# Inner products of a Strassen-Winograd FFN kernel on one core: one more third-level pair, two input tiles summed by a load, small operations and quarter products in another place

## The chip, the cores and the metric

The kernel runs on one core of a Trainium2 chip. Its engines work in parallel, each through its own list of instructions in order: TensorE (PE in the profile, with its weight loads as PEld) multiplies matrices into PSUM banks, VectorE (DVE) and GpSimd (POOL) do elementwise arithmetic, ScalarE (ACT) applies functions and copies, and SyncE (SP) only issues transfers. POOL issues transfers as well, by a queue of its own, and each such issue stands in POOL's list between its other instructions. Instructions of different engines wait for each other by semaphores. The metric is the device time of one execution, in microseconds (us); lower is better.

## The reference

The kernel computes two layers with residuals on x of shape (32, 128, 2048), float32. In each, a conditioned mixing of the channels feeds a feed-forward part:

```
def L0_cond(x, embedding, ...):
    att = softmax(mlp(embedding))                      # (32, 8)
    agg_w = einsum('bk,koi->boi', att, weight)
    agg_b = att @ bias_k
    return einsum('boi,bih->boh', agg_w, x) + agg_b[:, :, None]
def L0_ffn(x, W, bias, A, Bf, coeffs, scales):
    out = einsum('bsd,od->bso', x, W) + bias           # x as (32, 128, 2048), W (2048, 2048)
    return out + einsum('ebsr,eor,e->bso', einsum('bsd,erd->ebsr', x, A), Bf, coeffs * scales)
def L1_cond(x, c, weight, c_weight, bias):
    out = conv1d(x, weight, groups=4, taps=9)
    return out + (c @ c_weight.T)[:, :, None] + bias[None, :, None]
def L1_ffn(x, up, down, perm):
    t = x[..., perm] in 16 heads of 128
    return (gelu(t @ up[head]) @ down[head])[..., unperm]
x = x + L0_ffn(L0_cond(x, cond, ...), ...)
x = x + L1_ffn(L1_cond(x, cond, ...), ...)
```

What this case is about is the first large product, x with the 2048x2048 matrix W (into which the low-rank update of A and Bf has been added), for 32x128 = 4096 rows.

## The kernel before

**The product and its rounds.** The product of x and W is cut in halves on all three sides and done by a scheme of seven products in place of eight. The seven outer products are the rounds, in the order `ROUNDS` P1, P2, P6, P7, P5, P3, P4. Each needs one combination of W's quarters and one of x's. A round goes over 8 steps g = 0 to 7, one for each group of four batches, so there are 56 steps; "step 17" is round P6 with g = 1. Within a step the same scheme is used once more: the step's matrices are cut again, seven inner products, also named P1 to P7, are made, and each is added into the quarters of the step's result.

**One step on PE.** One inner product is four matmuls (128x128 weights by 128x512), which the profile shows as 8 records of one half each, 0.429 us apart; a product thus takes 3.43 us. A plain step, `multiply` (L331), makes all seven products. In the pairs of steps that `PAIRS` (L51) lists, `multiply_third` (L426) is used instead: each of the two steps makes five products itself (P1, P5, P6, P3, P7, at L445), and the remaining two of both steps together are made by a third level of the scheme, as seven "quarters" (L458), each of 8 records of 128x256. All quarters run in the pair's odd step. `turn` places them: with `early` true they come between the five products, two after P1, two after P5, two after P6, one after P3; with `early` false they come behind the five. In the rounds P1 and P4 (`ENDS`) they come behind, in the others between. After a pair's odd step, the results of both steps are stored from SP (L275). Pair numbers are g // 2.

**Reading of banks.** Each product accumulates in a PSUM bank. After P1 has been written, VectorE adds the bank into the step's results (L438 for the third-level step, one addition for each of up to two results); P6 and P7 go on accumulating in that same bank, so they may begin only when the addition before has read it. The quarters' additions are at L466.

**Inputs of a step.** `x_loads` (L283) issues the loads of x's tiles (1 MB each) from SP, two steps ahead at the top of a step; for steps of P6 at the fourth of the six calls of `between` in the step. `x_combine` (L294), one step ahead, makes the combination on POOL. Its `pieces` (L277) are four POOL operations of 128x512 each: for P6 it makes x10 + x11 and from this takes x00, which is eight operations, and stores the outcome to the scratch s2 by POOL's own queue; for P5 it makes x10 + x11 alone. Then follow four operations that make the inner combinations s (L309 to L312): s[0] is used by inner P5, s[1] by P6, s[2] by P7, s[3] by P3. Inner P1 uses the combination itself. The tiles live in a pool of 26 slots of 1 MB, and a load waits until its slot is free.

**Other work on POOL and VectorE.** `inner_weights` (L243), 16 POOL operations, makes a round's inner weights in the last step of the round before. `outer_weights` (L520) loads and combines a round's outer weights in steps g = 2 to 6 of the round before. `third_weights` (L378) makes the quarters' weights: part on POOL at the first pair of a round, the others (`quarter_ops`) on VectorE at calls of `between`. `third_inputs` (L410) makes the quarters' inputs sq by four operations; on VectorE in pair 0 of a round and in all pairs of P6, right after the even step, else on POOL in the even step (L1079). `mixed_kernel` (L553) puts two VectorE operations of the mixed weights into each of the first four calls of `between`.

**The loop.** One pass of the loop at L1068 issues step i. On POOL the order of a pass is: the combination of step i+1, sq if it is POOL's, the inner weights if g = 7, the outer combination. Then the step's products run, with `between(0)` to `between(5)` among them.

**The small chain.** `small()` (L876) computes softmax, the bias `aggb` (8 VectorE operations, L931 to L935), `ctxb` and `ctx34` (four small matmuls and five VectorE operations, L938 to L945), the scaled row sums and the convolution's weights, cut in parts by `yield`; each pass of the loop takes one part, from step 5 on two. `aggb` and `ctxb` are first read after the seven rounds.

After the rounds comes a phase with the layers' remaining parts and the 16 heads' FFN (from L1180), which the change does not touch.

Of the kernel before, what the change touches and what calls it, by code (L numbers as in the profile page):

```python
# [11 lines left out]
ALU = mybir.AluOpType  # L12
# [4 lines left out]
P = 128  # L17
B = 32
L = 2048
QW = 512  # L20
KEXP = 8
GR = 4
# [26 lines left out]


PAIRS = {  # L51
    "P1": (1, 2, 3), "P2": (0, 1, 2), "P6": (0, 1, 2, 3), "P7": (0, 1, 2, 3),
    "P5": (0, 1, 2, 3), "P3": (0, 1, 2, 3), "P4": (0,),
}
ENDS = ("P1", "P4")
# [3 lines left out]
def adaln_ffn_kernel(  # L59
# [16 lines left out]
    nc = tc.nc  # L76
# [12 lines left out]
    def bank():  # L89
        return banks.pop(0)  # L90

    def done(*ps):
        banks.extend(ps)

    def halves(t):
        return [t[:, r * NQ : (r + 1) * NQ] for r in range(2)]
# [23 lines left out]
    att_bc = const.tile([P, B * KEXP], FP, name="att_bc", tag="att_bc")  # L120
    aggb = const.tile([P, B], FP, name="aggb", tag="aggb")
    ctxb = const.tile([P, GR, B], FP, name="ctxb", tag="ctxb")
    ctx34 = const.tile([P, GR, B], FP, name="ctx34", tag="ctx34")
# [140 lines left out]
    def x_load(g, tp, kh):  # L264
        t = slot(f"xt_{g}{tp}{kh}", (P, 2, 2, QW))
        nc.sync.dma_start(t.rearrange("p k s c -> p (k s c)"), xT[g, tp, kh])
        return t
# [9 lines left out]
    def pieces(out, a, b, op):  # L277

        for i in range(2):
            for j in range(2):  # L280
                nc.gpsimd.tensor_tensor(out[:, i, j], a[:, i, j], b[:, i, j], op)  # L281

    def x_loads(r, g):  # L283
        return {
            "P1": lambda: [x_load(g, 0, 0)],
            "P2": lambda: [x_load(g, 0, 1)],
            "P6": lambda: [x_load(g, 1, 0), x_load(g, 1, 1), x_load(g, 0, 0)],
            "P7": lambda: [x_load(g, 0, 0), x_load(g, 1, 0)],
            "P5": lambda: [x_load(g, 1, 0), x_load(g, 1, 1)],
            "P4": lambda: [x_load(g, 1, 1)],  # L290
            "P3": lambda: [x_load(g, 0, 1), part_load("s2", g)],
        }[r]()

    def x_combine(r, g, ts):  # L294

        a = ts[0]
        tt = nc.gpsimd.tensor_tensor
        if r == "P6":

            b, a, c = ts  # L300
            pieces(b, b, a, ALU.add)
            pieces(a, b, c, ALU.subtract)
            part_store("s2", g, a)
        if r in ("P7", "P5", "P3"):
            pieces(a, a, ts[1], ALU.add if r == "P5" else ALU.subtract)
        xa[steps.index((r, g))] = a
        s = slot(f"s_{r}{g}", (P, 4, QW))
        a11, a12, a21, a22 = a[:, 0, 0], a[:, 1, 0], a[:, 0, 1], a[:, 1, 1]
        tt(s[:, 0], a21, a22, ALU.add)  # L309
        tt(s[:, 1], s[:, 0], a11, ALU.subtract)  # L310
        tt(s[:, 2], a11, a21, ALU.subtract)
        tt(s[:, 3], a12, s[:, 1], ALU.subtract)  # L312
        return {
            "P1": a11, "P2": a12, "P3": s[:, 3], "P4": a22,
            "P5": s[:, 0], "P6": s[:, 1], "P7": s[:, 2],
        }
# [109 lines left out]
    def multiply_third(r, g, lhs, rhs, olds, between, quarters, sq):  # L426

        px, py = bank(), bank()
        accs = olds if olds[0] is not None else [slot(f"m_{r}{g}", (P, 2, 2, QW))]
        fresh = set()  # L430
        if sq:
            both = [held.pop(), accs]

        def add(si, oi, ps):
            for acc in accs:
                to = acc[:, si, oi]
                if olds[0] is not None or (si, oi) in fresh:
                    nc.vector.tensor_tensor(to, ps, to, ALU.add)  # L438
                else:
                    nc.scalar.copy(to, ps)  # L440
            fresh.add((si, oi))

        def product(k, ps, first, last):
            for kc in range(4):
                nc.tensor.matmul(  # L445
                    ps, lhsT=lhs[k][:, bass.ts(kc, P)], rhs=rhs[k][kc],
                    start=first and kc == 0, stop=last and kc == 3, skip_group_check=True,
                )

        def quarter(k, to):  # L450

            if k in ("P1", "P5", "P2"):
                qs[k] = bank()
            ps = qs[{"P6": "P1", "P7": "P1", "P4": "P1", "P3": "P5"}.get(k, k)]
            first, last = k in ("P1", "P2", "P5"), k in ("P2", "P3", "P4")
            for i, out in enumerate(halves(ps)):
                for kc in range(2):
                    nc.tensor.matmul(  # L458
                        out, lhsT=sq[k][:, i, bass.ts(kc, P)], rhs=quarters[i][k][kc],
                        start=first and i == 0 and kc == 0, stop=last and i == 1 and kc == 1,  # L460
                        skip_group_check=True,
                    )
            b, h = to
            for acc in both[b]:
                part = acc[:, :, 0, h * NQ : (h + 1) * NQ]
                nc.vector.tensor_tensor(  # L466
                    part, ps.rearrange("p (s n) -> p s n", s=2), part, ALU.add
                )
            if last:
                done(ps)  # L470

        qs = {}
        turns = [
            (("P1", (0, 0)), ("P2", (0, 0))), (("P6", (0, 1)), ("P5", (1, 1))),
            (("P7", (1, 1)), ("P3", (0, 1))), (("P4", (1, 0)),),
        ]

        def turn(n, now):
            if sq and now:
                for k, to in turns[n]:  # L480
                    quarter(k, to)

        early = r not in ENDS
        product("P1", px, True, False)
        add(0, 0, px)
        between(0)
        turn(0, early)
        product("P5", py, True, False)
        add(1, 1, py)
        between(1)  # L490
        turn(1, early)
        product("P6", px, False, False)
        add(0, 1, px)
        between(2)
        turn(2, early)
        product("P3", py, False, True)
        add(0, 1, py)
        done(py)
        between(3)
        turn(3, early)  # L500
        product("P7", px, False, True)
        add(1, 1, px)
        add(1, 0, px)
        done(px)
        turn(0, not early)
        between(4)
        turn(1, not early)
        turn(2, not early)
        between(5)
        turn(3, not early)  # L510
        if not sq:
            held.append(accs)
            return
        for b, accs in enumerate(both):
            for (_, new), acc in zip(ADDED[r], accs):
                part_store(new, g - 1 + b, acc, nc.sync)
# [359 lines left out]
    def small():  # L876
# [7 lines left out]
        cond_s, w0, b0s, w1, b1s, w2, b2s, bk, cw, fb = (take(P, n) for _, n in SMALLS)  # L884
# [42 lines left out]
        nc.tensor.matmul(p3[:, : B * KEXP], lhsT=ones[0:B], rhs=adiag, start=True, stop=True)  # L927
        nc.vector.tensor_copy(att_bc, p3[:, : B * KEXP])
        done(p3)
        ab = att_bc.rearrange("p (b k) -> p b k", k=KEXP)  # L930
        nc.vector.tensor_scalar(aggb, ab[:, :, 0], bk[:, 0:1], None, ALU.mult)  # L931
        for k in range(1, KEXP):
            nc.vector.scalar_tensor_tensor(
                aggb, ab[:, :, k], bk[:, k : k + 1], aggb, ALU.mult, ALU.add
            )  # L935

        yield
        for r in range(GR):  # L938
            p4 = bank()
            nc.tensor.matmul(  # L940
                p4[:, :B], lhsT=cw[:, r * P : (r + 1) * P], rhs=cond_s, start=True, stop=True
            )
            nc.vector.tensor_scalar(ctxb[:, r], p4[:, :B], fb[:, r : r + 1], None, ALU.add)
            done(p4)
        nc.vector.tensor_scalar(ctx34, ctxb, 0.75, None, ALU.mult)  # L945
        yield

        while len(made) < 16:
# [58 lines left out]
        for g in range(NG):  # L1007
            nc.vector.tensor_scalar(orow[:, g], pos, g * L, None, ALU.add)
            if g % 2 == 1:
                yield  # L1010


    ctx.enter_context(tc.manual_schedule())
# [4 lines left out]
    steps = [(r, g) for r in ROUNDS for g in range(NG)]  # L1018
# [14 lines left out]
    xs = {0: [x_load(0, 0, 0)]}  # L1033
# [22 lines left out]
    rhs = inner_weights("P1", first, make_first)  # L1056
# [4 lines left out]
    nxt, waiting, ts, quarter_ops = {}, {}, {}, []  # L1061
# [6 lines left out]
    for i, (r, g) in enumerate(steps):  # L1068
# [13 lines left out]
        if i + 1 < len(steps) and not last_round and i != NG - 1:  # L1082
            olds_load(i + 1)
        ahead = i + 2 < len(steps) and ri > 0 and not last_round
        if ahead and steps[i + 2][0] != "P6":
            xs[i + 2] = x_loads(*steps[i + 2])
        if g == NG - (1 if ri else 2) and ri < len(ROUNDS) - 1:
            nxt = inner_weights(ROUNDS[ri + 1], [nxt[kc] for kc in range(4)])
# [36 lines left out]
        def between(j):  # L1125

            b = (ri - 1) * (NG - 2) + g + 1 if ri > 0 else g - (NG - 2)
# [6 lines left out]
                nc.vector.tensor_tensor(*quarter_ops.pop(0), ALU.subtract)  # L1134
            if i == NG - 1 and j == 3:
                olds_load(i + 1)
            if j == 3 and ahead and steps[i + 2][0] == "P6":
                xs[i + 2] = x_loads(*steps[i + 2])
            if ri == 0 and j in (1, 3) and unsummed:
                row_sums(*unsummed.pop())  # L1140
            if ri == 0 and j == 5 and unsummed_first:
                t = unsummed_first.pop(0)
# [33 lines left out]
        if g == NG - 1 and ri + 1 < len(ROUNDS):  # L1176
            rhs = nxt
# [3 lines left out]
    for k, (g, h) in enumerate(heads):  # L1181
# [5 lines left out]
        t = ts.pop(k)  # L1187
# [77 lines left out]
```

## Time and profile before

| quantity | value |
|---|---|
| median of three runs | 2590.43 us (2590.31 to 2591.47) |
| the profiled execution's own time | 2593.28 us |
| its span in the profile | 2591.5 us |
| mean granted PE clock | 0.998 |
| PE's idle time before L458, released by L466 | 3.3 us, once |
| PE's idle time before L221, released by L224 | 3.1 us in two waits, the longest 2.8 |
| a step of round P2 by `multiply` | 24.03 us |
| an even and an odd step by `multiply_third` | 17.17 and 29.25 us |

The span is one execution as the profiler recorded it, from its first to its last instruction; the execution's own time is a little longer than the span. A row of the profile names the line, the engine, the operation, then output and inputs with the tile names, and the number of instructions. A timeline row begins with the start in us from the span's beginning and the length of the group; in square brackets stand the idle time of that engine directly before it, and what ended it. A DMA row gives the size of a transfer and the median time from its issue to its landing. The two steps of a third-level pair differ in length because the odd one also runs the seven quarters.

### The profile page before, as it was taken

Reading aid. Unit: us, or ns where it says so; the run is one execution under the profiler, and the core shown is the slowest. Engines: PE = TensorE matmul, PEld = TensorE weight load, DVE = VectorE, ACT = ScalarE, POOL = GpSimd, SP = SyncE. Lnnn points to the kernel's source line nnn. Section 1 sums busy time; section 2 is a strip of 40 time slices with the busy share of each in tenths; the row PEclk is TensorE's granted clock in tenths of the full one; section 3 lists DMA queues with packets and bytes.
Section 4 is the critical chain, followed back from the end, with each engine's and each line's share of the span. In section 5 each row is a group of like instructions: output and inputs, shape, how many; then the busy total and the mean of one; then the engine's idle time right before and its main releaser. Section 6 shows DMA issues by size and latency. Waiting matters only on the chain. (4 is left out here: it accounts for less than half of the span.)

```text
span 2591.5 us, 21761 instructions
## 1 busy us (share of the span) xinstructions
PE 2576.1 (99%) x7022; PEld 1335.3 (52%) x7022; DVE 1512.9 (58%) x2373; ACT 532.4 (21%) x1099; POOL 1369.4 (53%) x1128
## 2 busy tenths in 40 slices
PE   9999999999999999999999999999999999999999
PEld 4455555455555555555554554555545554455543
DVE  5665565466555667544376666667666666666601
ACT  0000000000000000000011244444444444444432
POOL 7431766989977935968523234343444334434222
PEclk9999999999999999999999999999999999999999
DMA  7452458779366477474767788877777877787532
GB/s 324 177 211 97 179 219 325 280 311 365 158 258 284 164 316 321 181 311 163 247 233 247 241 299 263 250 238 230 223 234 236 258 231 221 226 256 233 162 128 89
DMA packets 186577, 608.30 MB, mean 235 GB/s; under 512 B 17632, under 2 KB 91872, under 8 KB 142304
## 3 DMA queue, kind: packets, MB, share of 16 engines
q1 hardware_dynamic: 147936, 473.48, 51.0%
q0 software_dynamic: 32704, 130.04, 14.9%
q10 hardware_dynamic: 5824, 3.40, 0.4%
q8 instruction: 56, 0.92, 0.1%
q14 instruction: 57, 0.47, 0.1%
HBM read 372.45 MB, written 200.84 MB: 221 GB/s over the span
## 5 line engine op out<-in xcount | busy, mean ns | idle before, releaser
L835 PE MATMUL bank<-t,ws 128*128 128x512 f32 x1024 | 460.3, 592 | 0.0
L846 PE MATMUL bank<-gl,ws 128*128 128x512 f32 x1024 | 460.1, 592 | 0.0
L853 POOL DMA_INDIRECT out<-t,orow x128 | 152.4, 1191 | 540.8 <-DVE t L851 472.2
L838 ACT ACTIVATE gl<-bank 128x512 f32<-128x512 f32 x512 | 305.9, 598 | 417.6 <-PE bank L835 414.4
L445 PE MATMUL bank<-P_t,s_P 128*128 128x512 f32 x736 | 326.6, 592 | 0.0
L846 PEld LDWEIGHTS bank<-gl,ws 128*128 128x128 f32 x1024 | 194.6, 190 | 233.0 <-issue 231.5
L835 PEld LDWEIGHTS bank<-t,ws 128*128 128x128 f32 x1024 | 194.6, 190 | 226.6 <-issue 222.9
L584 POOL TENSOR_TENSOR x<-x,fb 128x512 f32<-128x512 f32 x128 | 176.1, 1405 | 231.5 <-DMA x<-in_x 134.2
L851 DVE TENSOR_TENSOR t<-bank,t 128x512 f32<-128x512 f32 x128 | 88.4, 691 | 325.2 <-PE bank L846 325.2
L438 DVE TENSOR_TENSOR u<-bank,u 128x512 f32<-128x512 f32 x204 | 134.0, 687 | 239.3 <-PE bank L445 223.8
L590 ACT ACTIVATE bank<-w,aggb 128x512 f32<-128x512 f32 x128 | 80.8, 683 | 869.0 <-DMA w<-w_d 856.7
L445 PE MATMUL bank<-wo_P,s_P 128*128 128x512 f32 x544 | 241.6, 592 | 0.0
L281 POOL TENSOR_TENSOR xt<-xt,xt 128x512 f32<-128x512 f32 x128 | 164.0, 1314 | 113.6 <-DMA xt<-in_xT 113.6
L445 PEld LDWEIGHTS bank<-P_t,s_P 128*128 128x128 f32 x736 | 139.8, 190 | 159.8 <-issue 155.7
L563 DVE SCALAR_TENSOR_TENSOR ags<-mix,att_bc,ags 128x128 f32<-128x128 f32 x224 | 174.9, 781 | 4.7
L309 POOL TENSOR_TENSOR s_P<-xt 128x512 f32<-128x512 f32 x56 | 73.7, 1316 | 194.0 <-DMA xt<-in_xT 181.0
L445 PEld LDWEIGHTS bank<-wo_P,s_P 128*128 128x128 f32 x544 | 103.4, 190 | 116.5 <-issue 113.8
L819 POOL DMA_INDIRECT t<-hx_d,row x128 | 132.3, 1033 | 57.4 <-issue 24.9
L458 PE MATMUL bank<-P_q,sq 128*128 128x256 f32 x552 | 129.2, 385 | 3.4 <-DVE u L466 3.3
L458 PEld LDWEIGHTS bank<-P_q,sq 128*128 128x128 f32 x552 | 106.6, 194 | 35.6 <-issue 20.6
L438 DVE TENSOR_TENSOR p<-bank,p 128x512 f32<-128x512 f32 x84 | 56.7, 689 | 113.7 <-PE bank L445 113.7
L445 PE MATMUL bank<-wo_P,xt 128*128 128x512 f32 x272 | 122.3, 592 | 0.0
(190 smaller groups left out, 3525.6 us busy)
## 6 DMA issues: line engine op xcount, KB each, us to landing
xt<-in_xT SPq DMA_DIRECT2D x88, 1024.0 KB, 11.8
u<-u_d SPq DMA_DIRECT2D x40, 1024.0 KB, 10.2
wo_P<-wb_d SPq DMA_DIRECT2D x36, 1024.0 KB, 13.8
u<-c_d SPq DMA_DIRECT2D x64, 512.0 KB, 7.1
x<-in_x SPq DMA_DIRECT2D x32, 1024.0 KB, 9.2
xg<-x SPq DMA_DIRECT2D x256, 128.0 KB, 5.5
hx_d<-x1t SPq DMA_DIRECT2D x32, 1024.0 KB, 6.0
hx_d<-ht SPq DMA_DIRECT2D x32, 1024.0 KB, 7.2
```

What stands on the lines that cost most here:

```text
L281: nc.gpsimd.tensor_tensor(out[:, i, j], a[:, i, j], b[:, i, j], op)
L438: nc.vector.tensor_tensor(to, ps, to, ALU.add)
L445: nc.tensor.matmul(ps, lhsT=lhs[k][:, bass.ts(kc, P)], rhs=rhs[k][kc], start=first and kc == 0, stop=last and kc == 3, skip_group_check=True,)
L458: nc.tensor.matmul(out, lhsT=sq[k][:, i, bass.ts(kc, P)], rhs=quarters[i][k][kc], start=first and i == 0 and kc == 0, stop=last and i == 1 ...
L563: nc.vector.scalar_tensor_tensor(ag, mix[:, k], att, ag, ALU.mult, ALU.add)
L584: nc.gpsimd.tensor_tensor(xt[:, f], xt[:, f], late["fb"][:, f], ALU.add)
L819: nc.gpsimd.indirect_dma_start(out=t.rearrange("p k t -> p (k t)"), out_offset=None, in_=hx_d[g].rearrange("l k t -> l (k t)"), in_offset= ...
L835: nc.tensor.matmul(pu, lhsT=w[:, m * P : (m + 1) * P], rhs=t[:, 0], start=True, stop=True)
L838: nc.scalar.activation(gl[m], pu, AF.Gelu)
L846: nc.tensor.matmul(pd, lhsT=w[:, (MC + m) * P : (MC + m + 1) * P], rhs=gl[m], start=(m == 0), stop=(m == MC - 1),)
L851: nc.vector.tensor_tensor(t[:, 1], pd, t[:, 1], ALU.add)
L853: nc.gpsimd.indirect_dma_start(out=out, out_offset=bass.IndirectOffsetOnAxis(ap=orow[:, g, h : h + 1], axis=0), in_=t[:, 1], in_offset=None,)
```

## The change

There are four edits.

1. `PAIRS["P2"]` gets pair 3, so that steps g = 6 and 7 of round P2 go by `multiply_third`.
2. In P6 and P5, x10 + x11 is no longer made by POOL operations from two loaded tiles. x10 is loaded by SP; a transfer from POOL's queue then reads x11 from memory and adds it onto the loaded tile (`accum_op=add`). `x_add` puts this transfer into a list, which is issued at `between(1)`, that is behind the pass's other POOL work. P6 loads two tiles by SP in place of three and runs four pieces in place of eight; P5 loads one in place of two and runs none. P6's loads move from `between(3)` to the top of the step two ahead, where the others are.
3. The operations of `aggb`, `ctxb` and `ctx34` move to the end of `small()`, two at a time between `yield`s; what stood behind them comes one or two parts earlier.
4. `early` is false in all of P6 and wherever the pair's odd step has g = 1: the quarters of these pairs come behind the five products.

```diff
@@ -49,7 +49,7 @@
 PAIRS = {
-    "P1": (1, 2, 3), "P2": (0, 1, 2), "P6": (0, 1, 2, 3), "P7": (0, 1, 2, 3),
+    "P1": (1, 2, 3), "P2": (0, 1, 2, 3), "P6": (0, 1, 2, 3), "P7": (0, 1, 2, 3),
@@ -280,13 +280,21 @@
+    pending = []
+
+    def x_add(t, g, tp, kh):
+        pending.append(lambda: nc.gpsimd.dma_start(
+            t.rearrange("p k s c -> p (k s c)"), xT[g, tp, kh], accum_op=ALU.add
+        ))
+        return t
+
...
-            "P6": lambda: [x_load(g, 1, 0), x_load(g, 1, 1), x_load(g, 0, 0)],
+            "P6": lambda: [x_add(x_load(g, 1, 0), g, 1, 1), x_load(g, 0, 0)],
...
-            "P5": lambda: [x_load(g, 1, 0), x_load(g, 1, 1)],
+            "P5": lambda: [x_add(x_load(g, 1, 0), g, 1, 1)],
@@ -297,12 +305,10 @@
         if r == "P6":
 
-            b, a, c = ts
-            pieces(b, b, a, ALU.add)
-            pieces(a, b, c, ALU.subtract)
+            pieces(a, a, ts[1], ALU.subtract)
             part_store("s2", g, a)
-        if r in ("P7", "P5", "P3"):
-            pieces(a, a, ts[1], ALU.add if r == "P5" else ALU.subtract)
+        if r in ("P7", "P3"):
+            pieces(a, a, ts[1], ALU.subtract)
@@ -480,7 +486,7 @@
-        early = r not in ENDS
+        early = r not in ENDS and r != "P6" and g != 1
@@ -927,14 +933,79 @@
         nc.vector.tensor_copy(att_bc, p3[:, : B * KEXP])
         done(p3)
+        yield
...
         ab = att_bc.rearrange("p (b k) -> p b k", k=KEXP)
         nc.vector.tensor_scalar(aggb, ab[:, :, 0], bk[:, 0:1], None, ALU.mult)
         for k in range(1, KEXP):
             nc.vector.scalar_tensor_tensor(
                 aggb, ab[:, :, k], bk[:, k : k + 1], aggb, ALU.mult, ALU.add
             )
-
-        yield
+            if k % 2 == 1:
+                yield
         for r in range(GR):
...
             done(p4)
+            if r % 2 == 1:
+                yield
         nc.vector.tensor_scalar(ctx34, ctxb, 0.75, None, ALU.mult)
         yield
@@ -1082,7 +1091,7 @@
         ahead = i + 2 < len(steps) and ri > 0 and not last_round
-        if ahead and steps[i + 2][0] != "P6":
+        if ahead:
             xs[i + 2] = x_loads(*steps[i + 2])
@@ -1134,8 +1143,10 @@
-            if j == 3 and ahead and steps[i + 2][0] == "P6":
-                xs[i + 2] = x_loads(*steps[i + 2])
+            if j == 1:
+                for add in pending:
+                    add()
+                pending.clear()
```

More of the change, by code (lines that the diff above doesn't have):

```diff
@@ L929, in small @@
         done(p3)
[L930 to L935, printed above, removed]
-        yield
[L938 to L945, printed above, removed]
         yield
@@ L1010, in small @@
                 yield
+        ab = att_bc.rearrange("p (b k) -> p b k", k=KEXP)
+        nc.vector.tensor_scalar(aggb, ab[:, :, 0], bk[:, 0:1], None, ALU.mult)
+        for k in range(1, KEXP):
+            nc.vector.scalar_tensor_tensor(
+                aggb, ab[:, :, k], bk[:, k : k + 1], aggb, ALU.mult, ALU.add
+            )
+            if k % 2 == 1:
+                yield
+        for r in range(GR):
+            p4 = bank()
+            nc.tensor.matmul(
+                p4[:, :B], lhsT=cw[:, r * P : (r + 1) * P], rhs=cond_s, start=True, stop=True
+            )
+            nc.vector.tensor_scalar(ctxb[:, r], p4[:, :B], fb[:, r : r + 1], None, ALU.add)
+            done(p4)
+            if r % 2 == 1:
+                yield
+        nc.vector.tensor_scalar(ctx34, ctxb, 0.75, None, ALU.mult)
+        yield
     ctx.enter_context(tc.manual_schedule())
```

## The prediction

> **What bounds the kernel now.** First the page's busy table, to see which engine sets the time; then PE's waits, since only they can be removed on a busy PE; then DVE's and PE's timelines around the two long waits, the granted clock in windows there, and POOL's timeline where P6 begins.
>
> ```profile
> span 2591.5 us, 21761 instructions
> PE 2576.1 (99%) x7022; PEld 1335.3 (52%) x7022; DVE 1512.9 (58%) x2373; ACT 532.4 (21%) x1099; POOL 1369.4 (53%) x1128
> ```
> PE works 2576.1 of 2591.5 us: a change gains by fewer PE instructions or by its 15.4 us of idle time, and loses by any new wait of PE.
>
> ```profile
> PE bank L458 <- DVE u L466: 3.3, 1, 3.3
> PE bank L221 <- DVE w L224: 3.1, 2, 2.8
> ```
> Two waits (total, times, longest) are long. DVE's timeline (start, length) shows what was ahead of L224 for the second, PE's the first:
> ```profile
> 208.17 0.28 DVE L931 TENSOR_SCALAR aggb<-att_bc,small 128x32 f32<-128x32 f32 x1
> 208.48 4.97 DVE L933 SCALAR_TENSOR_TENSOR aggb<-att_bc,small,aggb 128x32 f32<-128x32 f32 x7
> ...
> 213.37 2.47 DVE L224 TENSOR_TENSOR w<-bank,w 128x512 f32<-128x512 f32 x4
> ```
> ```profile
> 884.33 3.60 PE L445 MATMUL bank<-P_t,s_P 128*128 128x512 f32 x8
> 891.25 6.47 PE L458 MATMUL bank<-P_q,sq 128*128 128x256 f32 x16 [3.33 <-DVE u L466]
> ```
> The windows around the latter (PE busy first, PEclk, the granted clock, third from the end):
> ```profile
> 885.00:890.00 5.00, 2.92 (x7) 0.95 (x5) 4.96 (x6) 0.00 (x0) 5.00 (x5) 1.00 0.14 57
> 890.00:895.00 5.00, 3.75 (x9) 3.06 (x10) 4.96 (x8) 0.00 (x0) 4.84 (x5) 0.51 0.00 2
> ```
> A wait costs more than its length: the clock halves behind it, record by record for 6.8 us here and 3.4 us behind the 2.8 us wait at 211. Waits of 0.46 to 0.88 show no drop. POOL where P6's first inputs are made:
> ```profile
> 458.07 9.82 POOL L281 TENSOR_TENSOR xt<-xt,xt 128x512 f32<-128x512 f32 x8 [14.83 <-DMA xt<-in_xT]
> ...
> 494.81 11.18 POOL L281 TENSOR_TENSOR xt<-xt,xt 128x512 f32<-128x512 f32 x8
> 506.29 0.57 POOL L275 DMA_DIRECT2D s_d<-xt  x1 [0.30 <-POOL xt L281]
> 506.88 1.27 POOL L309 TENSOR_TENSOR s_P<-xt 128x512 f32<-128x512 f32 x1
> ```
> ```profile
> 505.54 3.60 PE L445 MATMUL bank<-wo_P,xt 128*128 128x512 f32 x8
> ```
> Step 17 (P6, g=1) starts at 505.54 with P1; its P5 needs s0 of L309, done at 508.15, and is due at 508.98. POOL is 53% busy on the mean, but here has 0.8 us to spare.
>
> **The change, part by part.**
>
> *Third level in P2's last pair.* PE's timeline gives a plain pair 488.38 − 440.31 = 48.07 us and a third-level pair 393.89 − 347.47 = 46.42: gain **1.65**. Its sq costs POOL four operations of 1.27 = 5.1 us, startable when PE's last quarter of the pair before ends (436.9). It ends by 442, hidden under POOL's present 14.83 us wait to 458; without that cover all 5.1 would go into P6's chain below.
>
> *Biases at the end.* The 8 DVE operations (5.25 us) leave the place ahead of L224. Summing what PE's records take above the pitch there gives 2.96 for the wait and gap, 0.49 behind it, and three later 0.42: **4.7** gained. At their new place they come two by two, about 1.4 us of DVE at a step's end in steps 15 to 17, with four small matmuls that only change place. DVE (58% busy) hides them; uncovered, one pair delays a bank's reading by at most 1.4.
>
> *Late quarters.* At P5's g=1, wait and half clock exceed the pitch by 3.49+0.34+11×0.21+0.20 = 6.3. With quarters behind, PE runs P1, P5, then P6 at 884.33, which needs P1's two adds read. Those stand behind sq's four operations on DVE (1.11, 1.64, 1.76, 1.75; ended 886.19 in the timeline), so they end at 887.4: a residue of 3.0, and with the 2.6 of clock little gained (0.7). At the first operation's 1.11 each, sq ends at 884.5 and the adds at 885.7: residue 1.3, gain 5.0. I take **5.0**, as POOL's four pieces of P5 that ran beside sq are gone. P6's g=1 has three small excesses, 0.17+0.19+0.10 = **0.46**. In pair 0 of P2, P7 and P3 the P1 add is done 0.5, 0.5 and 0.8 us before P6 is due, so nothing there. Gains: 1.65+4.7+5.0+0.46 = **11.8**.
>
> *Load with addition.* In P5 four pieces of 1.3 us vanish, and s has 7 to 31 us to spare against PE there, so the addition may take long: nothing lost. In P6 four of eight pieces vanish (5.2 us per step), but the addition is issued on POOL's queue as the last thing of a step and the next instruction on POOL, the first piece of that same tile, needs it landed. So 5.2 us of work become L, issue to landing, with POOL idle, and behind the waiting piece stand s, the store of s2, sq's or inner weights' operations and the next outer combine: all that P6 gets. One removed SP load of 1024 KB per step frees its queue; the POOL queue gains 16 transfers and 16 issues of 0.57.
>
> No addition is in the trace. The nearest row is the s2 store: same queue, kind, size and stretch.
> ```profile
> s_d<-xt POOLq DMA_DIRECT2D x8, 1024.0 KB, 10.5
> xt<-in_xT SPq DMA_DIRECT2D x88, 1024.0 KB, 11.8
> ```
> ```profile
> DMA to landing us min/median/max: 4.4/10.6/18.6
> ```
> Bounds: 4.4, the store's best, and 21, twice 10.5, since the addition must also read the tile. I take L = 10.5, the row's median. The Trainium skill, "DMA: Bandwidth & Descriptors", in its rules for kernel authors, says to issue a DMA early, compute, and wait late; the change does the contrary in P6. Its bandwidth table gives 6.15 us for 1 MB from this queue; by that the loss below would be 2.6 and the time 2581. The row says 10.5 in this traffic, and decides.
>
> The chain of POOL with L, against PE running 1.65 earlier:
> - x10 of step 16 landed at 456 (first of three SP loads of that burst, issued 442.7): addition at 456+10.5 = 466.5; four pieces 4.9, store 0.9, s 5.0: 477.3; inner weights 21.0 (473.81 to 494.81 now): 498.3.
> - Step 17: addition at 508.8; first piece 510.1, where PE's P1 was due 503.9: wait 6.2. s0 at 508.8+4.9+0.9+1.3 = 515.9, where P5 is due 510.1+3.4 = 513.5: 2.4. Sq on DVE starts at the pieces' end 513.7, takes 6.7, then P1's add 0.6: 521.0, where P6 is due 519.3: 1.7. Together **10.2**.
> - From s0 to the next s0 POOL needs 3.9 (rest of s) + L + 7.1 = 21.5, five more where an outer combine lies between (steps 21, 22, 23), and 5.0+6.35+L+7.1 = 29.0 from step 17 to 18 (the first with inner quarters' operations, 6.35). PE allows 17.17 before an odd and 29.25 before an even step, so even steps catch up what odd ones lose. Carrying both sums forward leaves waits of 2.4 (step 19), 1.6 (step 21) and 6.6 (step 23), and none in even steps.
>
> Loss 10.2+2.4+1.6+6.6 = **20.8**. Half clock behind the two waits over 2.8: by the trace half of 3.4 to half of 6.8 each, mean 2.55: **5.1**. Net 20.8+5.1−11.8 = +14.1. The profiled execution's span of 2591.5 lies in 2593.28, against a median of 2590.43; the difference of 2.9 is the execution's own, so I put the net onto the median: 2590.4+14.1 = **2604.5**.
>
> The same sum for other L (loss with clock; time): 4.4 to 6.2: 2.6; 2581. 7: 6.6; 2585. 8: 8.6; 2587. 9: 11.5; 2590. 9.5: 18.0; 2597. 11: 32.6; 2611. 12: 43; 2622. 13: 51; 2630. 15: 67; 2646. 21: 120; 2699. So the sign turns at L = 9. Shorter than 4.4 would bring nothing more: the 2.6 left there are DVE's sq before the P1 add of odd steps, and PE has no wait in P6 beyond the 0.46 to remove.
>
> **Rivals.**
> A, the forecast: POOL waits for each addition and P6's odd steps starve. For it: 0.8 us spare now; seven of the eight stores took 9.1 to 11.3.
> B, the other side, faster: additions land in under 8.3 us because P6 has one SP load less per step and the addition starts after the burst of loads it waited for; POOL then gains or breaks even. For it: the store that went out at 529.75, between bursts, took 4.4. Against it: the seven others. Time 2581 to 2587, taken as 2584; it decides from L below 8.3.
> C, cancelling: L between 8.3 and 9.8: 2588 to 2599, about 2591. The bound for telling anything from no change is 0.2%, 5.2 us.
> D: the addition runs at half a copy's rate or in the middle of bursts, L of 13 and more: 2630 to 2660. For it: two reads and a write per element, and the store's worst of 18.6; also SP loads wait for slots that POOL frees, so a late POOL makes the second operand late.
> E, that the additions hide anyway: only if P6 needed its inputs late, and step 17's 0.8 us speaks against it. It is counted in B.
>
> **How the numbers follow.** A 0.46 (L 9.8 to 13), B 0.30, C 0.13, D 0.11. The predicted time is A's, 2604.5. A's own range is 2597 to 2630; the range for 8 in 10 runs from B's floor, 2580, to 2626, leaving out D and A's upper edge. Faster by over 0.2% (under 2585.2): most of B, 0.28. Within: the rest of B and most of C, 0.14. Slower (over 2595.6): A, D and C's end, 0.58.
>
> **What would show it.** Right: POOL's idle time before the first piece of steps 16 to 23 near 10 us, released by the addition's transfer and not by an SP load; PE waiting at L445 in steps 17, 19, 21, 23 for POOL's xt, s and DVE, with the longest at step 17; the PE clock at half behind the longest; P2's last pair at 46.4; no wait at 211 and one under 3 at 888. Wrong: additions landing in 6 to 8 us, with POOL's idle time as short; P6's steps still 17.17 and 29.25; an addition delayed by SP's loads instead; DVE late at steps 15 to 17 through the biases.

## The result and the profile after

The changed kernel takes 2633.74 us (median of five runs, 2633.19 to 2635.75) against 2590.43: a ratio of 1.0166, with a 95% interval of 1.0155 to 1.0178. It is slower by 43 us. The forecast was slower, but 2604.5, and its range ended at 2626.

The page of the changed kernel, busy time and instructions by engine:

```profile
span 2632.0 us, 21769 instructions
PE 2585.0 (98%) x7046; PEld 1340.1 (51%) x7046; DVE 1502.5 (57%) x2378; ACT 532.3 (20%) x1099; POOL 1301.2 (49%) x1084
```

POOL works 68 us less than before, and PE is idle for 47 us in place of 15. PE's waits in the changed kernel (total, times, longest):

```profile
PE bank L451 <- DVE p L444: 20.6, 5, 11.7
PE bank L451 <- POOL xt L281: 8.3, 3, 3.1
PE bank L451 <- POOL s_P L315: 2.6, 2, 2.1
```

The two waits of before (3.3 and 3.1 us) are gone from their places, and these have come, all but 0.5 us of them, 31.0 us, in round P6. Windows over this round, from the start of its first step to the start of P7's, show it whole; the columns are window, length, then busy us and records of PE, PEld, DVE, ACT and POOL, then PEclk, the granted clock. First the changed kernel, then the one before:

```profile
482.51:713.97 231.46, 200.49 (x554) 107.97 (x553) 103.95 (x154) 0.00 (x0) 150.91 (x128) 0.93 0.71 242
```
```profile
488.38:674.60 186.22, 186.19 (x546) 103.19 (x545) 112.15 (x143) 0.00 (x0) 170.58 (x140) 1.00 0.77 301
```

P6 begins 5.9 us sooner (482.51 against 488.38): that is what the third pair and the biases' place bring, but 0.9 us of it is the four small matmuls of `ctxb`, which stood ahead of P6 and now stand in it (L1011, the 8 records by which the two rows differ). Then P6 lasts 45.2 us longer: 31.0 us of idle PE (231.46 less 200.49), these 0.9 us, and 13.4 us by which the same matmuls take longer at the lower clock (200.49 less 186.19 is 14.3). The rest of the program adds about 1 us; the two spans are 40.5 us apart, since the profiled execution of before was 2.9 us over its median.

What P6 waits for is seen on POOL. Two additions of the changed kernel (L286) and the pieces behind them, from POOL's timeline:

```profile
540.48 0.88 POOL L286 DMA_DIRECT2D xt<-in_xT  x1
555.89 4.92 POOL L281 TENSOR_TENSOR xt<-xt,xt 128x512 f32<-128x512 f32 x4 [14.52 <-DMA xt<-in_xT]
...
567.94 0.90 POOL L286 DMA_DIRECT2D xt<-in_xT  x1
580.17 4.94 POOL L281 TENSOR_TENSOR xt<-xt,xt 128x512 f32<-128x512 f32 x4 [11.33 <-DMA xt<-in_xT]
```

POOL issues, and then waits 14.5 and 11.3 us for what it issued. The answer for that line, first with POOL's waiting at the pieces of the first eight (us, times), then over all 16 additions:

```profile
  POOL xt L281: 88.3, 8
...
DMA to landing us min/median/max: 7.9/12.2/15.3
```

POOL stands still for 88.3 us in P6 to save 8 x 5.2 = 42 us of arithmetic. But the largest of PE's waits names VectorE, and VectorE's own waits in P6 show a second row that the forecast did not have:

```profile
DVE sq L423 <- POOL wo_P L281: 25.5, 2, 15.8
DVE sq L423 <- POOL xt L281: 11.1, 2, 6.3
```
```profile
607.45 1.29 DVE L444 TENSOR_TENSOR p<-bank,p 128x512 f32<-128x512 f32 x2 [2.10 <-PE bank L451]
624.55 0.69 DVE L423 TENSOR_TENSOR sq<-xt 128x512 f32<-128x512 f32 x1 [15.82 <-POOL wo_P L281]
```

At steps 21 and 23 sq does not wait for its own inputs, whose pieces had ended at 613.7 and 670.4, but for the outer weights' combination that ends at 624.5 and 681.2. Nothing in the code joins them but the pool of 26 slots: sq gets the slot of the second outer weight, which that combination frees (e5 below gives sq another slot, and the wait is gone). The additions alone do not bring this about: the kernel before with them (e4) takes one tile less in each step of P6 too, and its sq waits there for POOL's xt alone.

### The profile page after: what moved, and what is told of

Same layout as the page of the kernel before. It is cut to its first block, busy times and chain, and to the rows that moved or that the text cites. A ratio compares the mean times of both kernels' runs of the same rounds, so it can differ in the third digit from the quotient of the medians.

```text
span 2632.0 us, 21769 instructions
## 1 busy us (share of the span) xinstructions
PE 2585.0 (98%) x7046; PEld 1340.1 (51%) x7046; DVE 1502.5 (57%) x2378; ACT 532.3 (20%) x1099; POOL 1301.2 (49%) x1084
## 5 line engine op out<-in xcount | busy, mean ns | idle before, releaser
L451 PE MATMUL bank<-P_t,s_P 128*128 128x512 f32 x768 | 348.6, 603 | 27.0 <-DVE p L444 20.6
L451 PEld LDWEIGHTS bank<-P_t,s_P 128*128 128x128 f32 x768 | 147.7, 194 | 208.3 <-issue 194.3
L569 DVE SCALAR_TENSOR_TENSOR ags<-mix,att_bc,ags 128x128 f32<-128x128 f32 x224 | 159.2, 711 | 4.7
L281 POOL TENSOR_TENSOR xt<-xt,xt 128x512 f32<-128x512 f32 x64 | 82.0, 1308 | 117.7 <-DMA xt<-in_xT 117.7
L444 DVE TENSOR_TENSOR p<-bank,p 128x512 f32<-128x512 f32 x96 | 64.6, 687 | 128.6 <-PE bank L451 126.1
L697 PE MATMUL bank<-va,tw_l 128*128 128x256 f32 x512 | 122.0, 380 | 1.9 <-DVE va L681 1.4
## 6 DMA issues: line engine op xcount, KB each, us to landing
wo_P<-wb_d SPq DMA_DIRECT2D x36, 1024.0 KB, 14.3
```

Of the source, the lines that this page charges most:

```text
L451: nc.tensor.matmul(ps, lhsT=lhs[k][:, bass.ts(kc, P)], rhs=rhs[k][kc], start=first and kc == 0, stop=last and kc == 3, skip_group_check=True,)
L569: nc.vector.scalar_tensor_tensor(ag, mix[:, k], att, ag, ALU.mult, ALU.add)
L697: nc.tensor.matmul(out, lhsT=w[:, 2 * i + r], rhs=rhs, start=first and r == 0, stop=last and r == 1, skip_group_check=True,)
```

## The experiments

### Without the additions

**e1** takes back the additions in P6 and P5 and leaves the other three edits.

```diff
-            "P6": lambda: [x_add(x_load(g, 1, 0), g, 1, 1), x_load(g, 0, 0)],
+            "P6": lambda: [x_load(g, 1, 0), x_load(g, 1, 1), x_load(g, 0, 0)],
-            "P5": lambda: [x_add(x_load(g, 1, 0), g, 1, 1)],
+            "P5": lambda: [x_load(g, 1, 0), x_load(g, 1, 1)],
...
```

> The changed kernel without its loads with addition: x10 + x11 of P6 and P5 is made on POOL from two loaded tiles, as before; the other three edits stay. Theory (the additions in P6 make the whole loss, and the other edits bring what the trace of after shows for them): step 16 starts 5.9 us earlier than before, P6 g=1 gives 0.5, P5 g=1 about 3 to 5, P7 g=1 loses 1.6, so the time is 2578 to 2584 us. Rival (the late quarters or the third pair cost part of the 43 us): above 2595.

Measured: 2603.03 us, ratio 1.0044 (1.0027 to 1.0061). The theory missed, and the rival's number held: the additions are not the whole loss, and the others cost 11 us. The rival's two suspects were not all of it, though. VectorE's waits in P6 of e1 and PE's:

```profile
DVE P_q L1145 <- POOL xt L281: 11.6, 1, 11.6
```
```profile
PE bank L453 <- DVE p L446: 10.6, 3, 9.2
```

A quarter's weight P_q waits 11.6 us for POOL's pieces of step 17: again a slot, it seems, this time one that those pieces free, and the additions of VectorE queued behind P_q hold PE for 9.2 us.

**e6** is e1 with that slot taken earlier, by a POOL instruction of 128x1 that writes into P6_q1 ahead of step 17's combination.

```diff
+                if r == "P6" and g == 0:
+                    t1 = slot("P6_q1", (P, 4, 2, NQ))
+                    nc.gpsimd.memset(t1[:, 0, 0, 0:1], 0.0)
                 lhs[i + 1] = x_combine(*steps[i + 1], xs.pop(i + 1))
...
```

> e1 (no additions, the other three edits) with the tile of the quarters' weights P6_q1 touched on POOL ahead of step 17's combination, so that its slot is not the one that this combination frees. In e1 VectorE waited 11.6 us there for POOL's pieces, PE 9.3 us, and the clock was halved behind it (2.4 us). Theory (the slot is the only thing that made e1 slower than before): 11 to 13 us less than e1, 2588 to 2592, and 2 to 6 us under before if P5's pair gives anything. Rival (the three edits cost something of their own): above 2596.

Measured: 2594.32 us, ratio 1.0007 (0.9998 to 1.0016). That is between the theory and the rival. The wait for the slot is gone, and it was worth 9 us of e1. But the three edits then gain nothing. The trace shows where the gain ahead of P6 goes: in the profiled execution, the slowest of its runs, P6 begins 5.6 us sooner than before (482.8) and lasts 193.1 us against 186.2, so that P7 begins 1.3 us later; in e7 below, with the same P6, it lasts 190.3. The next run shows what takes it.

**e8** is the kernel before with the late quarters alone (the one line with `early`).

> The kernel before with the late quarters alone. By the forecast 5.0 + 0.46 us are gained; by its lower bound for P5 g=1 (a residue of 3.0 us with 2.6 of clock) nothing. The trace of e1 has 3.2 us and five half-clock records of P5 g=1 in the late order, so 0 to 2 us gained: 2588 to 2591. Rival: 2585 or less.

Measured: 2597.78 us, ratio 1.0019 (1.0009 to 1.0029): slower by 4.9 us, which neither had. PE's waits in e8:

```profile
PE bank L445 <- DVE p L438: 3.4, 2, 2.0
PE bank L221 <- DVE w L224: 3.1, 2, 2.8
PE bank L445 <- DVE u L438: 3.1, 1, 3.1
```

The third row is P5's g = 1, as long as it was (3.3 before). The first row is new: it is P6's g = 1 and its last pair. P6 lasts 191.2 us here against 186.2, 3.4 us of idle PE and 1.6 of clock, and these 5.0 us are as much as e8's whole loss. VectorE's and PE's timelines in e8 show why:

```profile
506.83 1.88 DVE L417 TENSOR_TENSOR sq<-xt 128x512 f32<-128x512 f32 x1
508.75 1.64 DVE L418 TENSOR_TENSOR sq<-sq,xt 128x512 f32<-128x512 f32 x1
510.31 1.75 DVE L419 TENSOR_TENSOR sq<-xt,xt 128x512 f32<-128x512 f32 x1
511.99 1.75 DVE L420 TENSOR_TENSOR sq<-xt,sq 128x512 f32<-128x512 f32 x1
513.65 0.68 DVE L438 TENSOR_TENSOR p<-bank,p 128x512 f32<-128x512 f32 x1
```
```profile
508.86 3.60 PE L445 MATMUL bank<-P_t,s_P 128*128 128x512 f32 x8
514.48 5.37 PE L445 MATMUL bank<-P_t,s_P 128*128 128x512 f32 x8 [2.02 <-DVE p L438]
```

Whatever the order, sq stands on VectorE ahead of P1's addition. With the quarters in between, as before, the first that reads sq's sums comes 10.5 us after P1's start, and P6, which needs P1's addition read, 14.3 us after it (505.54, 516.03 and 519.86 in the kernel before). With the quarters behind, P6 comes after P1 and P5 alone, at 6.9 us. sq takes 6.8 us beside POOL, from 1.4 us after P1's start on. The wait of 2.0 is followed by 5.37 us for a product of 3.60: the granted clock is 0.52 from 514.48 to 518.00. Late quarters take away a wait for sq and shorten the time in which sq may run.

### The additions in P6

**e4** is the kernel before with the additions alone.

> The kernel before with the loads with addition alone. sq again shares a slot with the outer weights at steps 20 and 22, and the early quarters need sq right behind P1 and P5. Theory: the loss in P6 is as large as in after (45 us) or larger by a few us at each odd step, so 2635 to 2655. Rival (the loss needs the late quarters): under 2615.

Measured: 2621.95 us, ratio 1.0116 (1.0099 to 1.0133), 30 us; between the two. P6 lasts 217.0 us here, against 231.5 in the changed kernel, and begins 6.2 us later; P7 begins 8.3 us sooner (705.7 against 714.0). PE waits here for POOL itself:

```profile
PE bank L451 <- POOL xt L281: 19.0, 4, 9.1
```

**e2** and **e5** give sq another slot: in e2 by a POOL instruction of 128x1 behind the odd step's combination, in e5 ahead of it and in the last two pairs alone.

```diff
+                if r == "P6" and g in (4, 6):
+                    sqt = slot(f"sq_{i}", (P, 4, 2, NQ))
+                    nc.gpsimd.memset(sqt[:, 0, 0, 0:1], 0.0)
                 lhs[i + 1] = x_combine(*steps[i + 1], xs.pop(i + 1))
```

> The changed kernel, with one more POOL instruction of 128x1 at the top of P6's even steps that writes into sq before the outer combination, so that sq gets another slot of the pool and VectorE's sq no longer waits for POOL's outer combination at steps 21 and 23. In the trace of after PE waits 6.8 us at step 21 and 11.8 at step 23 for the additions behind that sq, with 2.7 and 3.3 us of halved clock. Theory A (POOL's chain of additions sets the pace; the slot only decides which engine is named): what PE no longer waits for sq it waits for POOL's xt and s, and the time falls by under 8 us, to 2626 or more. Theory B (the shared slot is a second cause): it falls by 10 to 25 us, to 2609 to 2624.

Measured: 2626.26 us, 1.0130 (1.0113 to 1.0146). That is at the edge of theory A, but the run did not decide, since its POOL instruction was itself waited for, 26.4 us by VectorE.

> The changed kernel with sq's slot taken by a POOL instruction of 128x1 ahead of the odd step's combination, in the last two pairs of P6 alone. In e2 that instruction stood behind the combination and was itself waited for (26.4 us of VectorE's time). Now VectorE's sq should wait only for the four pieces of its own step. Theory B (the shared slot is a cause of its own, beside the additions): the waits of 6.8 us at step 21 and 11.8 at step 23 shrink to under 3 each for sq, part of it comes back as a wait for POOL's xt or s at step 23, and the time is 2608 to 2622. Theory A (POOL's chain alone): above 2626.

Measured: 2628.83 us, 1.0135 (1.0120 to 1.0151). PE's waits in e5:

```profile
PE bank L452 <- POOL xt L281: 15.6, 4, 7.3
PE bank L452 <- POOL P_t L250: 4.8, 2, 3.1
PE bank L452 <- DVE p L445: 3.6, 5, 0.9
```

VectorE's row fell from 20.6 to 3.6 us, and POOL's xt rose from 8.3 to 15.6, with 4.8 of the next round's weights (P_t), which POOL now makes late. P7 begins 13.4 us sooner than in the changed kernel (700.6 against 714.0), but its first step takes 25.5 us instead of 17.1. The slot is worth 5 us by the medians (8 by the ratios), not the 17 by which VectorE's row fell: the chain on POOL sets the pace, and the slot in the main decided which engine PE named.

**e3** leaves the addition out of the 16 transfers: they overwrite the tile.

```diff
-            t.rearrange("p k s c -> p (k s c)"), xT[g, tp, kh], accum_op=ALU.add
+            t.rearrange("p k s c -> p (k s c)"), xT[g, tp, kh]
```

> The changed kernel with the addition left out of the 16 transfers: the same loads from POOL's queue overwrite the tile, so x11 stands where x10 + x11 belongs. If adding makes a transfer slow (it reads and writes the tile), these land in 8 to 10 us instead of 12.5 in the median, and the time falls by 10 to 20 us. If it is queue and traffic that make it slow, they land in 11 to 13 us and the time stays within 5 us of 2633.7.

Measured: 2605.79 us, 1.0048 (1.0031 to 1.0065), 28 us less, more than expected. The answer for the same line in e3, first over all 16 transfers, then over the eight of P6 (440 to 700 us), and last over those eight in the changed kernel:

```profile
DMA to landing us min/median/max: 5.2/6.1/11.8
```
```profile
DMA to landing us min/median/max: 5.3/8.8/11.8
```
```profile
DMA to landing us min/median/max: 8.1/12.4/15.3
```

With the same bytes from the same queue at the same places, the addition doubles the landing over all 16, 12.2 against 6.1 us. In P6, where POOL stands behind it, it makes 12.4 out of 8.8: there the overwriting load is slow as well. So e3's POOL still waits 67.1 us at the pieces of P6, against 88.3.

**e11** issues each addition at the top of the step, ahead of the inner weights and the outer combination.

```diff
             xs[i + 2] = x_loads(*steps[i + 2])
+        for add in pending:
+            add()
+        pending.clear()
```

> The changed kernel with each addition issued at the top of the step, behind the combination of step i+1 and ahead of the inner weights and the outer combination, where it was behind them. If the loss is the landing of an addition that nothing covers, covering it helps: step 17 has 21 us of inner weights behind its addition, so its 8 to 9 us of wait and half clock go; at steps 21 to 23 the outer combination covers 5 us of each landing. But POOL now waits there for SP's load of x10 first. Theory: 12 to 25 us less than after, 2608 to 2622. Rival (the place of the issue does not matter, or the wait for the load takes back what is covered): 2628 or more.

Measured: 2597.13 us, 1.0022 (1.0013 to 1.0031): 37 us less, more than expected, with the same 16 additions (7.7, 10.3 and 13.4 us to land, the least, the median and the most). PE's largest wait in e11 lies before P6:

```profile
PE bank L464 <- DVE p L472: 6.7, 1, 6.7
```

**e12** leaves step 16's addition at its old place and the others early (`if r == "P6" or g == NG - 1` ahead of the loop).

> e11 with the addition for step 16 at its old place, behind step 14's outer combination; the additions of P6's other steps stay early. In e11 POOL waited 16.2 us for the load of x10 there, and the outer combination then ran in one burst with step 16's pieces, just where VectorE had the mixed weights and the first biases: one VectorE operation of 128x128 that takes 0.35 us elsewhere took 9.2 us, until POOL's last piece, and PE waited 6.9 us behind it. Theory (the burst of POOL work held VectorE): that wait is gone, 7 to 8 us less than e11, 2588 to 2591, so that the additions, once early, leave nothing of the 43 us and the time stands at the kernel before. Rival (another wait takes its place at step 15 or 16): above 2594.

Measured: 2609.83 us, 1.0066 (1.0052 to 1.0079). The rival won. The wait at step 15 is gone, and PE comes to P6 9 us sooner than in e11, ahead of POOL again:

```profile
PE bank L451 <- DVE p L444: 12.8, 6, 6.3
PE bank L451 <- POOL s_P L315: 2.7, 2, 2.1
PE bank L451 <- POOL xt L281: 2.4, 1, 2.4
```

PE pays 9 us in e11 (6.7 of waiting, the rest of clock) in one piece before P6, and in e12 it waits inside P6 instead. But this is not the whole difference, for P7 begins at 680.7 in e11 and only at 692.5 in e12: POOL itself is slower there. It starts the pieces of step 17 3.0 us later than in e11 (495.7 against 492.8) and those of step 23 10.8 us later (644.4 against 633.6). Over half of that comes with one landing, step 19's; the pieces behind it in e11 and in e12, from POOL's timelines (cut at 545 and 552 us):

```profile
543.00 2.49 POOL L281 TENSOR_TENSOR xt<-xt,xt 128x512 f32<-128x512 f32 x2 [8.24 <-DMA xt<-in_xT]
```
```profile
549.47 3.70 POOL L281 TENSOR_TENSOR xt<-xt,xt 128x512 f32<-128x512 f32 x3 [13.99 <-DMA xt<-in_xT]
```

Why that landing was longer is open. Against the changed kernel, the earlier issue is worth 24 us with step 16's addition at its old place (e12), and 37 with all of them early (e11).

### What remains good

**e7** is e6 with the additions in P5. **e9** is e7 with the early quarters of before, **e10** is e9 without any addition: the third pair and the biases' place, with the touch of P6_q1.

> e6 with the additions kept in P5 alone. P5 has 7 to 31 us to spare at s, so additions of 8 to 15 us cost nothing there, and the four pieces that ran on POOL beside VectorE's sq are gone: sq's four operations shorten, PE's wait at P5 g=1 falls from 3.2 us to about 2, with no half clock behind it. Expected 2 to 4 us under e6, so 2584 to 2589. Rival (additions cost in P5 too): above e6.

Measured: 2593.26 us, 1.0004 (0.9995 to 1.0013). That misses the range; against e6 the difference is too small to tell.

> e7 with the early quarters of the kernel before (third pair in P2, biases at the end, additions in P5 alone, the tile of P6_q1 touched early). The late order cost e7, by its trace, 1.2 us at P6 g=1, 1.0 at P6's last pair and 4.4 at P5 g=1 (2.1 of wait, 1.7 of half clock, 0.6 at the quarters). In the early order P5 g=1 waits for sq, which without POOL's pieces beside it ends some 2 us sooner than before, so 0 to 2 us of wait and no half clock. Theory (the late order costs, the biases' place and the third pair gain): 3 to 6 us under e7, 2587 to 2590, a ratio to before of 0.996 to 0.999. Rival (what is gained is given back in round P4, where e7's PE has 3 us more of waiting than before's): a ratio of 0.999 to 1.001.

Measured: 2585.06 us, 0.9972 (0.9961 to 0.9982): 7 us faster than before, the best of all; the ratio is in the range expected. VectorE's and PE's timelines at P5's g = 1 in e9:

```profile
879.28 1.21 DVE L428 TENSOR_TENSOR sq<-xt,sq 128x512 f32<-128x512 f32 x1
880.41 1.28 DVE L446 TENSOR_TENSOR u<-bank,u 128x512 f32<-128x512 f32 x2
```
```profile
884.06 3.69 PE L466 MATMUL bank<-P_q,sq 128*128 128x256 f32 x16 [0.73 <-DVE u L474]
```

The wait that was 3.33 us is 0.73, and the quarters behind it keep full clock (16 records in 3.69 us against 6.47). P1 starts at 872.7 here, so sq ends 7.8 us after it (880.5), against 8.8 before (886.2 less 877.4), and the two mixed-weight operations behind it take 1.1 us in place of 2.6. Before, four pieces of POOL ran beside sq's first half (876.89 to 882.28) and four more beside the second of those operations (from 888.50); here POOL has none.

> e9 without any addition: the third pair in P2 and the biases' place alone (with the touch of P6_q1). The traces show step 16 starting 5.9 us earlier by these two. P5 g=1 then waits as before (6.3 us). Theory: 2 to 6 us under before, ratio 0.998 to 0.999, and above e9 by 2 to 5 us. Rival: given back in P4, ratio 1.000 or more.

Measured: 2589.74 us, 0.9991 (0.9982 to 1.0000): 2.3 us gained, of 5.9 seen up to P6 in the changed kernel. In e10's own trace PE is still 6.2 us ahead of before late in round P4 (1405.22 against 1411.38) and 3.8 us after that round (1502.10 against 1505.87); the two spans are 3.9 us apart. The 2.4 us between are lost at three places where PE waits and before did not:

```profile
1420.45 1.13 PE L699 MATMUL bank<-va,tw_l 128*128 128x256 f32 x4 [0.47 <-DVE va L683]
1471.03 1.13 PE L699 MATMUL bank<-va,tw_l 128*128 128x256 f32 x4 [0.49 <-DVE va L683]
1483.13 3.67 PE L843 MATMUL bank<-t,ws 128*128 128x512 f32 x8 [0.47 <-DMA ws<-in_ffw]
```

Ahead of the second, VectorE waits longer for a gather of x; VectorE's waits from 1330 to 1500 us, in e10 and in the kernel before:

```profile
DVE vb L680 <- DMA xg<-x: 3.6, 1, 3.6
```
```profile
DVE vb L672 <- DMA xg<-x: 0.7, 1, 0.7
```

So a part of what is gained ahead of P4 ends in such waits; the third is for a load of the heads' weights. No run removes them; the rest of the way from 3.9 to 2.3 us is within what single executions differ by.

## Why the prediction was wrong

The direction and the place were right: POOL waits for each addition in P6, PE starves there, the clock halves behind it, and the loss is larger than the gains. The size was not. The step that failed first is the sentence "I take L = 10.5, the row's median": the additions took 12.2, and 12.4 in P6. The forecast's own table gives 2622 at L = 12, still inside its range; gains that did not come make the rest. The store was the nearest row, but it does not add; e3 shows that in P6 the same transfer without the addition lands in 8.8, below the store, and that adding makes 12.4 of it. The upper bound, twice a store, was too wide. One reading of that row was wrong as well: the 18.6 called the store's worst belongs to the loads of s2 from SP, which the row counts too; the eight stores took 4.4 to 11.3.

The second is the late quarters: "I take 5.0" at P5 and 0.46 at P6. From e10 to e7, which adds them and P5's additions, the ratio rises from 0.9991 to 1.0004, a loss of 3.4 us where 5.5 were to be gained. At P5 the reasoning held in the changed kernel, with a residue of 1.9 us in place of 1.3. But at P6, where 0.46 was to be gained, the late order alone costs 5.0 us (e8). P6's g = 1 was counted as a gain without the question that had been asked of P5: is P1's addition read when P6 is due? It was asked for pair 0 of P2, P7 and P3 alone, and from a timing in which sq was not late; at P7's g = 1 1.5 us of waiting came too. With 4.0 us that the third pair and the biases did not bring (6.35 against 2.3), 2622 becomes 2622 + 8.9 + 4.0 = 2635, against 2633.7. So close a sum is partly luck, as the points below show.

Point by point:
- *Third pair and biases*: 6.35 forecast, 5.9 seen at the start of P6, of which 0.9 is only moved into P6; two new delays, 0.6 us each in P1 and P2, are most of what is missing. Only 2.3 us are left at the end (e10). That a later stage takes part of a gain was not in the forecast.
- *P5's additions*: "nothing lost" holds, and with the early quarters they gain 4.9 us by the ratios of e10 and e9 (0.9991 and 0.9972).
- *POOL's chain in P6*: its sum is right in kind. Worked again with L = 12 it asks for 33 us of waits and 10 of clock, and 31.0 and 13.4 were measured; but step by step it is off. Step 17 was to wait longest, 13 us, and waited 4.0, since step 16's x10 had landed at 448.9, not 456, and step 17's own addition took 8.1; steps 21 and 23 waited 11.5 and 11.7, in place of 5 and 10, with the slot's share in them. That the totals agree so well is partly luck.
- *The slot of sq*: not foreseen. It is named by 25.5 us of VectorE's waiting and worth 5 to 8 us (e5).
- *Half clock*: 13.4 us in P6, where the sum counted it behind waits of over 2.8 us alone; shorter ones can do it: behind the wait of 2.5 us at step 19 and of 2.1 at step 21 the granted clock is 0.59 and 0.52 for 3.5 us. It is not length alone, for at step 21 a wait of 2.7 us stands just ahead of the one of 2.1, and the product between them ran at full clock.
- *Rivals*: B (landing under 8.3 us) and E (hidden) are out, and C with them. D named 13 us and more, 2630 to 2660: the time fell there, with L a little under it; by the forecast's table L alone would have left it at some 2624, so D's number was met through the other losses too.

In ratios to the kernel before: third pair and biases 0.9991; P5's additions with the early quarters a further 0.998; late quarters, alone, 1.0019; P6's additions, from e7 to the changed kernel, 1.0004 to 1.0166, some 42 us; this step also moves P6's loads and takes e7's touch of P6_q1 away. Of these 28 are the price of adding in flight (e3), and 24 to 37 could be covered by issuing sooner (e12, e11); the two overlap. The 42 are no fixed price of the additions: on the kernel before they cost 30 (e4). There PE comes to P6 6.2 us later and sq waits for no outer weight; where POOL sets the pace, what PE has saved ahead of it turns into waiting.

## What to carry to other kernels

An arithmetic step that moves into a transfer is paid by its landing wherever its reader stands directly behind its issue: 5.2 us of work a step became 11.0 us of idle POOL (88.3 over 8), on an engine that had 0.8 us to spare there. Issue it ahead of other work or keep it where there is slack, as P5 shows. When a kernel takes fewer or more tiles from a pool, look again at which slot each later tile gets: a tile of one stage may wait for another that nothing else joins it to. And a product order that removes one wait shortens the cover of another; every accumulation that reads a bank in the new order has to be asked the same question.

## What the hardware showed that was not expected

- A load of 1024 KB from POOL's queue that adds onto its tile lands in 12.2 us (median of 16, 7.9 to 15.3), one that overwrites in 6.1 (5.2 to 11.8). It depends on the traffic: in P6 the medians are 12.4 and 8.8. The Trainium skill, "DMA: Bandwidth & Descriptors", in its section on bandwidth, states 6.15 us for 1 MB from this queue: the overwriting load's median over the 16 agrees, its median in P6 and the adding load do not.
- Issuing it takes 0.89 us on POOL, against 0.58 for the overwriting one.
- A wait of under 2 us can halve the clock, or not. At P5's g = 1 PE waits 1.9 us in the changed kernel and in e7; behind it, in windows of the changed kernel and then of e7, PEclk (third from the end) is 1.00 and 0.50:

```profile
927.50:931.00 3.50, 3.36 (x8) 1.63 (x9) 3.14 (x6) 0.00 (x0) 3.42 (x6) 1.00 0.02 5
```
```profile
885.00:888.40 3.40, 3.40 (x6) 1.34 (x5) 2.52 (x5) 0.00 (x0) 3.40 (x6) 0.50 0.02 7
```

The Trainium skill, "TensorE: Matmul & The Clock Gate", in its section on what is actually happening, describes a free-running window of 3.4 us, and says that the point at which the clock changes depends on where in the window the first matmul lands. That the same wait had two outcomes here fits this, but the wait is shorter than the idle window that the page names for half clock.
- In e11 VectorE stood still beside POOL's work. The timelines of VectorE and of POOL there:

```profile
450.47 9.62 DVE L569 SCALAR_TENSOR_TENSOR ags<-mix,att_bc,ags 128x128 f32<-128x128 f32 x2
```
```profile
449.44 10.09 POOL L281 TENSOR_TENSOR wo_P<-wo_P,wo_P 128x512 f32<-128x512 f32 x8
```

Two small operations that take 0.73 us together elsewhere took 9.62. The first of them took 9.23 and ended at 459.7, just behind POOL's eight pieces (459.5). The Trainium skill, "SBUF — State Buffer", in its section on the two separate sides, says that these two engines share a pair of ports as an exclusive lock held for a whole instruction, against a VectorE operation with two inputs in SBUF, as this one has; here VectorE stood still for nearly eight in a row. It is not so behind every such run: beside the eight pieces from 494.81 on in the kernel before, VectorE's operations took 0.69 to 1.79 us. That the port is the cause was not tried apart.
